# Three of seven block products of a mixture-of-experts second layer, taken one level deeper

## The chip, the cores and the metric

The kernel runs on one core of one Trainium2 chip. The metric is the device time of one launch in microseconds (us); less is better. A core has a matrix engine (TensorE, PE in the profile, with its weight loads as PEld), a vector engine (VectorE, DVE), a scalar engine (ScalarE, ACT), GpSimd (POOL) and SyncE (SP), which only issues transfers here. Each runs its own instructions in order, and they wait for each other by semaphores. On-chip data lies in SBUF, matmul results in banks of PSUM.

## The reference

A pre-norm block: attention with sine and cosine features, then a mixture of eight experts (E = 8) with the top two chosen for each token. Only the second half matters here. Every expert has room for 160 rows of each of 8 sequences, 1280 rows:

```python
h = jax.nn.relu(jnp.einsum('enc,ech->enh', buf, W1) + b1[:, None, :])   # C 512 -> H 2048
y = jnp.einsum('enh,ehc->enc', h, W2) + b2[:, None, :]                   # H 2048 -> C 512
y_tok = y.reshape(E * B * cap, C)[flat_idx.reshape(-1)].reshape(B, T * K, C)
y_tok = y_tok * (p_flat * keep.astype(x.dtype))[:, :, None]
return y_tok.reshape(B, T, K, C).sum(axis=2)
```

All of it is float32. The result is added to the residual x.

## The kernel before, in words

The first 1260 us are attention, normalisation and routing, which the change does not touch. Then come 16 chunks, two for each expert: even chunks (i = 0, 2, ...) of 768 rows (nh = 3) and odd chunks of 512 rows (nh = 2). A chunk is cut into two halves of rows, an upper and a lower one of nh blocks of 128 rows each, so that block number `block` of both halves can be handled together.

Both expert layers multiply 2 x 2 block matrices with seven products instead of eight (Strassen's scheme in Winograd's form). In the second layer the left matrix is `hid`: rows in two halves, the hidden 2048 in two halves of 1024 (NHQ = 8 pieces of 128). The right matrix is W2, 1024 + 1024 by 256 + 256 (DC = 256). The seven left operands and the seven right operands, called *parts* and *weights* 0 to 6, are made ahead by sums on VectorE: for the left side at the end of layer 1 (`p4`, lines 1280 to 1287), for the right side in `mix_w2` (lines 1066 to 1069).

`layer2(i, block, ...)` forms the two output tiles of one block, one from each half of the rows. Its `product` (line 1317) is a chain of 8 matmuls of 128 x 128 by 128 x 256 into one bank. The banks `top` and `mid` are accumulated over several products, and ScalarE copies or VectorE sums take what is needed from between (lines 1343 to 1369). Each finished row tile is multiplied by its gate on ScalarE (line 1329) and added to `out` in memory by an indirect transfer from POOL (line 1332). After each product, `next(aside)` advances `gather(i + 1)`, a generator that brings the rows of the next chunk: its transfers, a VectorE transpose for each tile of 128 rows (line 1175), and four sums (lines 1185 to 1188).

Layer 1 runs over q = 0 to 7. Each step has seven products p1 to p7 (line 1241), whose results ScalarE copies (lines 1251 to 1274) and whose weights are mixed by `mix_w1` (line 1214). p6 adds to the bank that p1 filled, so it needs ScalarE's copy of p1 (line 1251) first.

The order on TensorE, ScalarE, VectorE and SP is the order of the program text: `tc.manual_schedule` names these four engines. Tiles come from pools; a new tile of a pool with all its buffers taken waits for the last reader of the oldest. `hp` holds eight `hid` tiles, `w2p` eight tiles of W2, `yp` three row tiles y, `ps_p` six banks.

## Time and profile before

| | us |
|---|---|
| median of three runs | 3238.44 (3238.36 to 3239.85) |
| the profiled execution's own time | 3225.94 |
| its span, first to last instruction | 3224.2 |
| TensorE busy / VectorE / ScalarE / POOL | 3155.2 / 1936.5 / 1609.3 / 425.8 |
| mean granted clock of TensorE | 0.996 |
| second layer of an odd chunk (1712.70 to 1761.10) | 48.4 |
| second layer of an even chunk (1591.50 to 1664.30) | 72.8 |

The profile shows one execution. Busy times of engines overlap, so their sum is more than the span. [...] In a group line, the numbers after the bar are the busy time of the group in us, the mean length of one instruction in ns, and the idle time of the engine before them. In a timeline line they are start, length, engine, source line, operation, and how many were merged; what stands in brackets is the wait before and what ended it. In a line of stretches, each engine has its busy time and count, in the order PE, PEld, DVE, ACT, POOL, followed by the clock of TensorE, the share of the transfer engines, and GB/s.

### The profile page before, as it was taken

The numbers are of one execution on the slowest core, as the hardware profiler recorded it, in microseconds if no ns is written. First come the engines' busy times: TensorE is split into PE (matmuls) and PEld (weight loads), VectorE is DVE, ScalarE is ACT, GpSimd is POOL, SyncE is SP. The second block draws the span as 40 slices with busy tenths as digits, with TensorE's granted clock in tenths as the row PEclk, the third lists the DMA queues.
The fourth block names the chain that finished last, engine by engine and source line by source line (L and its number), as shares of the span: only waits on it lengthen the run. The fifth ranks groups of instructions, "written<-read, shape, count | busy, mean of one in ns | idle before, by whom it ended". The sixth has DMA issues, their size and how long they took to land.

```text
span 3224.2 us, 48128 instructions
## 1 busy us (share of the span) xinstructions
PE 3155.2 (98%) x18646; PEld 2136.9 (66%) x18646; DVE 1936.5 (60%) x4088; ACT 1609.3 (50%) x2289; POOL 425.8 (13%) x387
## 2 busy tenths in 40 slices
PE   5999999999999999999999999999999999999998
PEld 2444444444444445688688688688688688688687
DVE  8888888788787685634634634634634634634632
ACT  7888888888888875322322322322322322322322
POOL 3000202011111213311011011011011011011010
PEclk9999999999999999999999999999999999999999
DMA  5435454553545352434323333334333333334321
GB/s 165 145 99 164 133 147 141 146 157 106 184 106 158 96 165 87 129 78 108 121 66 104 122 66 104 123 64 106 122 66 102 123 66 103 123 66 104 119 46 20
DMA packets 288531, 358.52 MB, mean 111 GB/s; under 512 B 28376, under 2 KB 199088, under 8 KB 276272
## 3 DMA queue, kind: packets, MB, share of 16 engines
q1 hardware_dynamic: 264944, 312.20, 32.6%
q0 software_dynamic: 22912, 43.22, 7.5%
q8 instruction: 148, 2.42, 0.3%
q14 instruction: 79, 0.65, 0.1%
q10 hardware_dynamic: 448, 0.02, 0.0%
HBM read 207.02 MB, written 81.22 MB: 89 GB/s over the span
## 4 chain that ended last, share of the span: by engine, by line
PE 80%; DVE 3%; ACT 1%; issue 1%; DMA 0%; SPq 0%; POOLq 0%; DVEq 0%; ACTq 0%
PE ps_p L1241 30%; PE ps_p L1317 30%; PE av L717 9%; PE ps_s L683 9%; ACT e L703 1%; PE ps_s L215 1%; DVE qk_f L524 1%; PE ps_s L697 1%; DVE qk_r L447 0%; DMA qk<-qk_r 0%; DVE xT L837 0%; PE ps_s L874 0%; SPq L608 0%; PE ps_s L857 0%; DMA out_dram<-y,slots 0%
## 5 line engine op out<-in xcount | busy, mean ns | idle before, releaser
L703 ACT ACTIVATE e<-ps_s 128x1024 f32<-128x1024 f32 (+1 forms) x640 | 569.7, 937 | 184.2 <-PE ps_s L683 110.1
L683 PE MATMUL ps_s<-qk 64*128 64x512 f32 (+3 forms) x3072 | 598.1, 506 | 28.5 <-DMA qk<-qk_r 12.4
L1317 PE MATMUL ps_p<-w,hid 128*128 128x256 f32 x2560 | 575.9, 380 | 2.9 <-DVE w L1067 2.7
L1317 PEld LDWEIGHTS ps_p<-w,hid 128*128 128x128 f32 x2560 | 485.9, 190 | 74.9 <-DVE w L1067 7.6
L717 PE MATMUL av<-e,v 128*64 128x512 f32 (+3 forms) x3072 | 523.4, 490 | 0.0
L1317 PE MATMUL ps_p<-w_t,hid 128*128 128x256 f32 x1920 | 436.0, 380 | 0.5 <-DVE y L1366 0.5
L683 PEld LDWEIGHTS ps_s<-qk 64*128 64x128 f32 x3072 | 262.5, 188 | 216.2 <-issue 106.9
L1317 PEld LDWEIGHTS ps_p<-w_t,hid 128*128 128x128 f32 x1920 | 366.2, 191 | 51.1 <-DVE y L1366 0.9
L717 PEld LDWEIGHTS av<-e,v 128*64 128x64 f32 x3072 | 200.5, 137 | 283.0 <-issue 267.1
L1329 ACT ACTIVATE y<-y,slots 128x512 f32<-128x512 f32 x80 | 57.7, 722 | 524.5 <-DVE y L1362 448.2
L1241 PE MATMUL ps_p<-xe,w 128*128 128x256 f32 (+1 forms) x1024 | 317.6, 433 | 1.1 <-issue 1.1
L1241 PE MATMUL ps_p<-xe_s,t 128*128 128x256 f32 (+1 forms) x1024 | 318.2, 433 | 0.0
L1241 PE MATMUL ps_p<-xe,t 128*128 128x256 f32 (+1 forms) x1024 | 317.6, 433 | 0.0
L1332 POOL DMA_INDIRECT out_dram<-y,slots x80 | 127.4, 1593 | 1214.2 <-ACT y L1329 1055.6
L768 POOL DMA_INDIRECT slot_d<-token,slot x128 | 156.8, 1225 | 988.7 <-issue 612.2
L1241 PEld LDWEIGHTS ps_p<-xe_s,t 128*128 128x128 f32 x1024 | 193.7, 190 | 82.6 <-ACT hid L1251 1.6
L1241 PEld LDWEIGHTS ps_p<-xe,t 128*128 128x128 f32 x1024 | 194.2, 190 | 80.4 <-issue 0.4
L1241 PEld LDWEIGHTS ps_p<-xe,w 128*128 128x128 f32 x1024 | 194.2, 190 | 79.7 <-issue 1.2
L1343 DVE TENSOR_TENSOR y<-y,ps_p 128x256 f32<-128x256 f32 x40 | 16.9, 421 | 367.3 <-issue 191.4
L1284 DVE TENSOR_TENSOR hid<-hid 128x256 f32<-128x256 f32 (+1 forms) x128 | 64.0, 500 | 280.9 <-ACT hid L1282 280.9
L1241 PE MATMUL ps_p<-xe_s,w 128*128 128x256 f32 (+1 forms) x512 | 158.9, 433 | 0.6 <-ACT p L1257 0.6
L1251 ACT COPY hid<-ps_p 128x256 f32<-128x256 f32 (+1 forms) x128 | 54.3, 424 | 180.4 <-PE ps_p L1241 170.8
(229 smaller groups left out, 3640.6 us busy)
## 6 DMA issues: line engine op xcount, KB each, us to landing
w<-in_L_ffn_W_dram SPq DMA_DIRECT2D x256, 256.0 KB, 3.4
w<-in_L_ffn_W_dram SPq DMA_DIRECT2D x64, 512.0 KB, 8.1
qk<-qk_c SPq DMA_DIRECT2D x124, 256.0 KB, 4.4
qk<-qk_r SPq DMA_DIRECT2D x120, 256.0 KB, 4.8
qk_base<-base_d SPq DMA_DIRECT2D x28, 1024.0 KB, 7.7
xn_d<-xn SPq DMA_DIRECT2D x72, 256.0 KB, 2.4
rows_d<-xg SPq DMA_DIRECT2D x70, 256.0 KB, 2.1
x_mid<-in_L_attn_x_dram SPq DMA_DIRECT2D x16, 1024.0 KB, 8.9
```

Source lines behind the costliest of these rows:

```text
L215: nc.tensor.transpose(turned[:, a, :], src[r, :], ident[r, r])
L524: nc.vector.scalar_tensor_tensor(cols(p), ps[:, a, :].rearrange("p (t q) -> p t q", q=64), inv_qk[:, i * NCH + c : i * NCH + c + 1], cols( ...
L683: nc.tensor.matmul(ps[:, a, at : at + w], lhsT=pair[r, 1, kb * P : (kb + 1) * P], rhs=pair[r, 0, q0 : q0 + w], start=at == 0, stop=not own ...
L703: nc.scalar.activation(e, ps[:, :, :n], AF.Exp, scale=UNIT * UNIT / math.sqrt(2 * DH))
L717: nc.tensor.matmul(av[a * 64 : (a + 1) * 64, q0 - 512 * h :], lhsT=vt[:, kb, 2 * pr + a, :], rhs=es[i][:, a, at : at + w], start=kb == 0, ...
L768: queued = nc.gpsimd.indirect_dma_start(out=slot_d[b], out_offset=bass.IndirectOffsetOnAxis(ap=idx, axis=0), in_=src, in_offset=None,)
L1241: nc.tensor.matmul(ps, lhsT=weights[:, k, :], rhs=rows[:, k, :], start=first and k == 0, stop=last and k == 1, skip_group_check=True,)
L1251: nc.scalar.copy(self.blocks[0], self.top)
L1284: TT(g1, g3, h22, ALU.add)
L1317: nc.tensor.matmul(ps, lhsT=hs[k][:, part, cols], rhs=ws[k][weight], start=first and k == 0, stop=last and k == NHQ - 1, skip_group_check= ...
L1329: nc.scalar.activation(ys[r], ys[r], AF.Identity, scale=meta[:, e, jj[r], 1:2].bitcast(F32))
L1332: ins = nc.gpsimd.indirect_dma_start(out=out, out_offset=bass.IndirectOffsetOnAxis(ap=meta[:, e, jj[r], 0:1], axis=0), in_=ys[r], in_offse ...
```

## The change

For every chunk but the first, blocks 0 and 1 of the second layer are now handled together by a new function `layer2_quad`; block 2 of even chunks, and all of chunk 0, go through `layer2` as before. The pair has the same seven products, each for 256 rows. Four of them (0, 4, 5 and 6) stay plain: two chains of 8 matmuls with 256 columns. The other three (`SECOND`: part and weight 1, 2, and 3 with 6) are each cut into 2 x 2 blocks once more (rows 128 + 128, the inner 1024 in 512 + 512, columns 128 + 128) and done with seven chains of four matmuls with 128 columns. The sums of the operands, eight of 128 x 512, are made on VectorE by `mix`; ScalarE and VectorE combine the seven results in a tile c of four 128 x 128 blocks, which VectorE then adds to y. The order is: mix 0, products 0 and 4, second level 0, mix 1, product 5, second level 1, mix 2, product 6, second level 2.

The operand sums and c need room: in odd chunks the columns of `hid` that 512 rows leave free, in even chunks the tiles xe and xe_s, between their use by layer 1 and the next gather. So that slices can span pieces, `hid` and W2 become one tile each (all eight pieces), with the same transfers and sums. `yp` has four tiles instead of three. The gate of a lower row tile is applied to its two halves apart. In odd chunks the first mix of the next chunk's W1 comes before second level 2, and the gather's eight steps hang on the pair: two after product 0, two in each second level; in even chunks they hang on block 2.

```diff
     def load_w2(e):
-        w2_tiles[e] = []
+        w = w2_tiles[e] = pools["w2p"].tile([P, NHQ, 2, D], F32, name="w2")
         for k in range(NHQ):
-            w = pools["w2p"].tile([P, 2, D], F32, name="w2")
-            nc.sync.dma_start(w, src[:, :, k, :])
-            w2_tiles[e].append(w)
+            nc.sync.dma_start(w[:, k, :, :], src[:, :, k, :])
             yield
...
     def layer2(i, block, hid, aside):
...
+        gate(0, y1)
+        send(0, y1)
...
         TT(y22, y22, high, ALU.add)
+        gate(1, y22)
         product(top, 3, 6, False, True)
         TT(y21, top, low, ALU.add)
-        send(1)
+        gate(1, y21)
+        send(1, y2)
...
+    SECOND = [(1, 1), (2, 2), (3, 6)]
+
+    def layer2_quad(i, hid, aside, before_last):
...
+        def mix(n):
...
+            t1, t2, t3, t4, s2, s3, s4 = free[:7]
+            TT(t1, b12, b11, ALU.subtract)
+            TT(s3, a11, a21, ALU.subtract)
+            TT(a21, a21, a22, ALU.add)
+            TT(t2, b22, t1, ALU.subtract)
+            TT(s2, a21, a11, ALU.subtract)
+            TT(t3, b22, b12, ALU.subtract)
+            TT(s4, a12, s2, ALU.subtract)
+            TT(t4, b21, t2, ALU.subtract)
+            return (
+                (a11, b11), (a12, b21), (s4, b22), (a22, t4), (a21, t1), (s2, t2), (s3, t3)
+            )
...
+        def chain(ps, pair, first):
+            for k in range(4):
+                nc.tensor.matmul(
+                    ps, lhsT=pair[0][:, k, :], rhs=pair[1][:, k, :], start=first and k == 0,
+                    stop=k == 3, skip_group_check=True,
+                )
+
+        def second_level(n, pairs):
+            m1, m2, m3, m4, m5, m6, m7 = pairs
+            c = free[7 + n]
+            c11, c12, c21, c22 = (c[:, k, :] for k in range(4))
+            u, v, z = (bank()[:, :P] for _ in range(3))
+            chain(u, m1, True)
+            nc.scalar.copy(c11, u)
+            next(aside, None)
+            chain(v, m5, True)
+            nc.scalar.copy(c21, v)
+            chain(u, m6, False)
+            nc.scalar.copy(c12, u)
+            chain(z, m2, True)
+            TT(c11, c11, z, ALU.add)
+            chain(u, m7, False)
+            nc.scalar.copy(c22, u)
+            next(aside, None)
+            chain(v, m3, False)
+            TT(c22, c22, c21, ALU.add)
+            TT(c12, c12, v, ALU.add)
+            chain(u, m4, False)
+            nc.scalar.copy(c21, u)
+            return [c[:, 2 * b : 2 * b + 2, :] for b in two]
...
+        pairs = mix(0)
+        top, mid = bank(), bank()
...
+        product(top, 0, 0, True, False)
+        for b in two:
+            nc.scalar.copy(y11[b], of(top, b))
+            next(aside, None)
+        product(mid, 4, 3, True, True)
+        c = second_level(0, pairs)
+        for b in two:
+            TT(as_pair(y11[b]), as_pair(y11[b]), c[b], ALU.add)
+        pairs = mix(1)
+        product(top, 5, 4, False, False)
+        for b in two:
+            nc.scalar.copy(y12[b], of(top, b))
+            TT(y12[b], y12[b], of(mid, b), ALU.add)
+        c = second_level(1, pairs)
+        for b in two:
+            TT(as_pair(y12[b]), as_pair(y12[b]), c[b], ALU.add)
+        pairs = mix(2)
+        for b in two:
+            TT(y1[b], y1[b], b2_tiles[e], ALU.add)
+            gate[b](0, y1[b])
+            send[b](0, y1[b])
+        y2, y21, y22 = zip(*(new_y() for _ in two))
+        for b in two:
+            nc.scalar.copy(y22[b], of(mid, b))
+        product(top, 6, 5, False, True)
+        for b in two:
+            TT(y22[b], y22[b], of(top, b), ALU.add)
+            TT(y21[b], of(top, b), low, ALU.add)
+            TT(y22[b], y22[b], high, ALU.add)
+            gate[b](1, y22[b])
+        before_last()
+        c = second_level(2, pairs)
+        for b in two:
+            TT(as_pair(y21[b]), as_pair(y21[b]), c[b], ALU.add)
+            gate[b](1, y21[b])
+            send[b](1, y2[b])
...
     def experts(ending):
-        pools["hp"] = to_end.pool("hp", NHQ, **right)
+        pools["hp"] = to_end.pool("hp", 1, **right)
...
+            def mix_next():
+                if i + 1 < len(chunks):
+                    mix_w1(i + 1, 0)
+
+            if i:
+                layer2_quad(
+                    i, hid, iter(()) if nh > 2 else aside, mix_next if nh == 2 else lambda: None
+                )
+            for block in range(2 if i else 0, nh):
+                if block == nh - 1:
+                    mix_next()
+                layer2(i, block, hid, aside)
```

More of the change, by code (lines that the diff above doesn't have):

```diff
@@ L1052, in load_w2 @@
         src = W2[e].rearrange("(h k p) c -> p h k c", p=P, h=2)
-        w2_tiles[e] = []
+        w = w2_tiles[e] = pools["w2p"].tile([P, NHQ, 2, D], F32, name="w2")
         for k in range(NHQ):
-            w = pools["w2p"].tile([P, 2, D], F32, name="w2")
-            nc.sync.dma_start(w, src[:, :, k, :])
-            w2_tiles[e].append(w)
+            nc.sync.dma_start(w[:, k, :, :], src[:, :, k, :])
             yield
     def mix_w2(e):
-        for k, w in enumerate(w2_tiles[e]):
-            t = pools["w2p"].tile([P, 3, DC], F32, name="w2_t")
-            b11, b12 = w[:, 0, :DC], w[:, 0, DC:]
-            b21, b22 = w[:, 1, :DC], w[:, 1, DC:]
-            TT(t[:, 1, :], b12, b22, ALU.subtract)
-            TT(b12, b12, b11, ALU.subtract)
-            TT(t[:, 0, :], b22, b12, ALU.subtract)
-            TT(t[:, 2, :], b21, t[:, 0, :], ALU.subtract)
-            w2_tiles[e][k] = [b11, b21, b22, b12, t[:, 0, :], t[:, 1, :], t[:, 2, :]]
+        w = w2_tiles[e]
+        t = pools["w2p"].tile([P, NHQ, 3, DC], F32, name="w2_t")
+        b11, b12 = w[:, :, 0, :DC], w[:, :, 0, DC:]
+        b21, b22 = w[:, :, 1, :DC], w[:, :, 1, DC:]
+        t2, t3, t4 = (t[:, :, n, :] for n in range(3))
+        w2_tiles[e] = [b11, b21, b22, b12, t2, t3, t4]
+        for k in range(NHQ):
+            TT(t3[:, k, :], b12[:, k, :], b22[:, k, :], ALU.subtract)
+            TT(b12[:, k, :], b12[:, k, :], b11[:, k, :], ALU.subtract)
+            TT(t2[:, k, :], b22[:, k, :], b12[:, k, :], ALU.subtract)
+            TT(t4[:, k, :], b21[:, k, :], t2[:, k, :], ALU.subtract)
             yield
@@ L1220, in preln_attn_moe_kernel, with __init__ @@
     class Hidden:
-        def __init__(self, i, q, parts, asides):
+        def __init__(self, i, q, parts, hid, asides):
             e, j0, nh = chunks[i]
@@ L1227, in __init__ @@
             self.rows = parts
-            h = pools["hp"].tile([P, 7, HALF], F32, name="hid")
-            self.tile = h
-            self.blocks = [h[:, k, : self.n] for k in range(7)]
+            self.blocks = [hid[:, q, k, : self.n] for k in range(7)]
             self.low, self.high = (
@@ L1304, in layer1, with outputs, gate, send @@
         return this
-    def layer2(i, block, hs, aside):
+    def outputs(i, block):
         e, j0, nh = chunks[i]
+        jj = [j0 + block, j0 + nh + block]
+        def gate(r, part):
+            nc.scalar.activation(
+                part, part, AF.Identity, scale=meta[:, e, jj[r], 1:2].bitcast(F32)
+            )
+        def send(r, y):
+            ins = nc.gpsimd.indirect_dma_start(
+                out=out,
+                out_offset=bass.IndirectOffsetOnAxis(ap=meta[:, e, jj[r], 0:1], axis=0),
+                in_=y, in_offset=None, compute_op=ALU.add,
+            )
+            if i == 0:
+                tc.keep_in_program_order(ins)
+        return gate, send
+    def new_y():
+        y = pools["yp"].tile([P, D], F32, name="y")
+        return y, y[:, :DC], y[:, DC:]
+    def layer2(i, block, hid, aside):
+        e = chunks[i][0]
         ws = w2_tiles[e]
@@ L1317, in product @@
                 nc.tensor.matmul(
-                    ps, lhsT=hs[k][:, part, cols], rhs=ws[k][weight],
+                    ps, lhsT=hid[:, k, part, cols], rhs=ws[weight][:, k, :],
                     start=first and k == 0, stop=last and k == NHQ - 1, skip_group_check=True,
@@ L1321, in product @@
             next(aside, None)
-        jj = [j0 + block, j0 + nh + block]
-        ys = [pools["yp"].tile([P, D], F32, name="y") for _ in jj]
-        (y11, y12), (y21, y22) = ((y[:, :DC], y[:, DC:]) for y in ys)
+        gate, send = outputs(i, block)
+        (y1, y11, y12), (y2, y21, y22) = new_y(), new_y()
         low, high = b2_tiles[e][:, :DC], b2_tiles[e][:, DC:]
-        def send(r):
-            nc.scalar.activation(
-                ys[r], ys[r], AF.Identity, scale=meta[:, e, jj[r], 1:2].bitcast(F32)
-            )
-            ins = nc.gpsimd.indirect_dma_start(
-                out=out,
-                out_offset=bass.IndirectOffsetOnAxis(ap=meta[:, e, jj[r], 0:1], axis=0),
-                in_=ys[r], in_offset=None, compute_op=ALU.add,
-            )
-            if i == 0:
-                tc.keep_in_program_order(ins)
         def side_product():
@@ L1361, in layer2 @@
         TT(y12, y12, mid, ALU.add)
-        TT(ys[0], ys[0], b2_tiles[e], ALU.add)
-        send(0)
+        TT(y1, y1, b2_tiles[e], ALU.add)
+        gate(0, y1)
+        send(0, y1)
         if plain_first:
@@ L1367, in layer2, with places @@
         TT(y22, y22, high, ALU.add)
+        gate(1, y22)
         product(top, 3, 6, False, True)
         TT(y21, top, low, ALU.add)
-        send(1)
+        gate(1, y21)
+        send(1, y2)
+    def places(i, hid):
+        if chunks[i][2] == 2:
+            return [
+                hid[:, 4 * half : 4 * half + 4, part, 2 * P : 3 * P]
+                for part in range(7) for half in range(2)
+            ]
+        xe = pools["xep"].tile([P, NCH, 2, HALF], F32, name="xe")
+        s = pools["xep"].tile([P, 3, 2, HALF], F32, name="xe_s")
+        return [
+            t.rearrange("p a b n -> p (a b n)")[:, k * D : (k + 1) * D].rearrange(
+                "p (k n) -> p k n", n=P
+            )
+            for t, count in ((xe, 6), (s, 4))
+            for k in range(count)
+        ]
@@ new lines, in preln_attn_moe_kernel, with split, bank, as_pair @@
+    SECOND = [(1, 1), (2, 2), (3, 6)]
+    def layer2_quad(i, hid, aside, before_last):
+        e = chunks[i][0]
+        ws = w2_tiles[e]
+        free = places(i, hid)
+        low, high = b2_tiles[e][:, :DC], b2_tiles[e][:, DC:]
+        two = range(2)
+        def split(t, part_of):
+            return [[part_of(t[:, 4 * k : 4 * k + 4], c) for c in two] for k in two]
+        def mix(n):
+            part, weight = SECOND[n]
+            a = split(hid, lambda t, c: t[:, :, part, c * P : (c + 1) * P])
+            b = split(ws[weight], lambda t, c: t[:, :, c * P : (c + 1) * P])
+            (a11, a21), (a12, a22) = a
+            (b11, b12), (b21, b22) = b
+            t1, t2, t3, t4, s2, s3, s4 = free[:7]
[9 more added lines that the diff above has]
+                (a11, b11), (a12, b21), (s4, b22), (a22, t4), (a21, t1), (s2, t2), (s3, t3)
+            )
+        def bank():
+            return pools["ps_p"].tile([P, 512], F32, name="ps_p")
+        def chain(ps, pair, first):
[3 more added lines that the diff above has]
+                    stop=k == 3, skip_group_check=True,
+                )
+        def second_level(n, pairs):
[21 more added lines that the diff above has]
+            return [c[:, 2 * b : 2 * b + 2, :] for b in two]
+        def as_pair(t):
+            return t.rearrange("p (c n) -> p c n", n=P)
+        def product(ps, part, weight, first, last):
+            for b in two:
+                for k in range(NHQ):
+                    nc.tensor.matmul(
+                        ps[:, b * DC : (b + 1) * DC],
+                        lhsT=hid[:, k, part, b * P : (b + 1) * P], rhs=ws[weight][:, k, :],
+                        start=first and k == 0, stop=last and k == NHQ - 1,
+                        skip_group_check=True,
+                    )
+        gate, send = zip(*(outputs(i, b) for b in two))
+        pairs = mix(0)
+        top, mid = bank(), bank()
+        of = lambda ps, b: ps[:, b * DC : (b + 1) * DC]
+        y1, y11, y12 = zip(*(new_y() for _ in two))
+        product(top, 0, 0, True, False)
[30 more added lines that the diff above has]
+        c = second_level(2, pairs)
+        for b in two:
+            TT(as_pair(y21[b]), as_pair(y21[b]), c[b], ALU.add)
+            gate[b](1, y21[b])
+            send[b](1, y2[b])
@@ L1398, in experts @@
             parts, box = box[0], [None]
-            hs, tiles = [], None
+            hid = pools["hp"].tile([P, NHQ, 7, HALF], F32, name="hid")
+            tiles = None
             ahead = rows_ahead(i + 1) if i and i + 1 < len(chunks) else iter(())
@@ L1409, in experts @@
                 next(ahead, None)
-                tiles = layer1(Hidden(i, q, parts, [ending]), tiles, q == NHQ - 1)
-                hs.append(tiles.tile)
+                tiles = layer1(Hidden(i, q, parts, hid, [ending]), tiles, q == NHQ - 1)
                 if i == 0 and q == NHQ // 2:
@@ L1414, in experts @@
                     to_router.close()
-                    for name, bufs in (("w2p", NHQ), ("yp", 3), ("bp", 1)):
+                    for name, bufs in (("w2p", 1), ("yp", 4), ("bp", 1)):
                         pools[name] = to_end.pool(name, bufs, reuse_waits="tile", **left)
@@ L1430, in experts @@
                 aside = behind(2, aside)
-            for block in range(nh):
-                if block == nh - 1 and i + 1 < len(chunks):
+            def mix_next():
+                if i + 1 < len(chunks):
                     mix_w1(i + 1, 0)
-                layer2(i, block, hs, aside)
+            if i:
+                layer2_quad(
+                    i, hid, iter(()) if nh > 2 else aside, mix_next if nh == 2 else lambda: None
+                )
+            for block in range(2 if i else 0, nh):
+                if block == nh - 1:
+                    mix_next()
+                layer2(i, block, hid, aside)
             rest(aside)
```

## The prediction

> **What bounds the kernel now.** I read the page's busy shares and chain first, then the waits after 1420 us, where the expert stage runs undisturbed.

> ```profile
> PE 3155.2 (98%) x18646; PEld 2136.9 (66%) x18646; DVE 1936.5 (60%) x4088; ACT 1609.3 (50%) x2289; POOL 425.8 (13%) x387
> ...
> PE ps_p L1241 30%; PE ps_p L1317 30%; PE av L717 9%; PE ps_s L683 9%; ACT e L703 1%; PE ps_s L215 1%; DVE qk_f L524 1%; PE ps_s L697 1%; DVE qk_r L447 0%; DMA qk<-qk_r 0%; DVE xT L837 0%; PE ps_s L874 0%; SPq L608 0%; PE ps_s L857 0%; DMA out_dram<-y,slots 0%
> ```
> ```profile
> PEld ps_p L1317 <- DVE w L1067: 3.0, 7, 0.4
> ...
> PEld ps_p L1241 <- ACT hid L1251: 1.6, 8, 0.2
> ```

> TensorE is the bound: the two product lines hold 60% of the chain, and in 1800 us its weight loads wait 4.6 us in all. So every microsecond of matmul removed counts in full, and so does every wait that the change gives TensorE. Its price per instruction comes from the timeline:

> ```profile
> 1602.15 3.62 PE L1317 MATMUL ps_p<-w,hid 128*128 128x256 f32 x16
> 1605.60 0.38 PE L1317 MATMUL ps_p<-w_t,hid 128*128 128x256 f32 x1
> ```
> ```profile
> 1289.00 0.60 PE L828 MATMUL ps_t<-ident,xn 128*128 128x128 f32 x4
> ```
> ```profile
> 1292.12 0.41 PEld L857 LDWEIGHTS ps_t<-gather_e,lg 128*128 128x128 f32 x3
> ```

> Sixteen instructions fill 1602.15 to 1605.60: 0.216 us each at 256 columns. They are one block product, so each of the 8 matmuls of the code is two instructions (4480 in all for 40 blocks x 7 x 8). At 128 columns four take 0.60; the last one's own length is 0.27, so they start 0.109 apart. Full f32 weight loads behind tiny matmuls start (0.41-0.19)/2 = 0.11 apart.

> [...] here load and matmul would both need about 0.11 us and overlap. [...]

> ```profile
> 1350.90:1354.30 3.40, 1.84 (x7) 0.64 (x5) 3.19 (x9) 0.00 (x0) 1.55 (x2) 1.00 0.80 208
> 1354.30:1361.10 6.80, 5.66 (x13) 4.04 (x14) 3.35 (x9) 0.37 (x1) 0.00 (x0) 0.52 0.67 216
> ...
> 1289.40:1292.80 3.40, 2.67 (x19) 1.83 (x20) 2.59 (x6) 1.17 (x2) 1.77 (x3) 1.00 0.27 94
> ```

> The first number after the length is TensorE busy, the third from the end the clock. 1.56 us idle in one window cost 6.8 us at half clock, that is 3.4 us of work; 0.73 us idle cost none. [...]

> **What goes and what comes on TensorE.** Chunks 1 to 15 each get one pair by layer2_quad: 15 pairs, three products each, 45. Plain, such a product is 32 instructions x 0.216 = 6.91 us; second level it is 7 chains x 8 x 0.109 = 6.10 us (a chain 0.872). 0.81 x 45 = **36 us gained**. Bounds: at 0.112 each, 29 us; if load and matmul did not overlap at all (0.19), 56 x 0.08 x 45 = 200 us lost. The seven waits for L1067 go, since its product now starts 3.5 us later: about 2 us gained.

> **VectorE's price and its cover.**

> ```profile
> L1214 DVE TENSOR_TENSOR t<-w,t 128x256 f32<-128x256 f32 x244 | 102.9, 422 | 4.2
> ...
> L1175 DVE STREAM_TRANSPOSE xe<-z 128x512 f32<-128x512 f32 x32 | 33.5, 1084 | 0.0
> ...
> L1187 DVE TENSOR_TENSOR xe_s<-xe 128x768 f32<-128x768 f32 x7 | 6.7, 958 | 0.2
> ...
> L1185 DVE TENSOR_TENSOR xe_s<-xe 128x512 f32<-128x512 f32 x8 | 5.5, 693 | 0.3
> ```

> Starts lie closer than lengths: in the timeline 0.61 us apart at 512 (3209.26 and 3209.87) and 0.34 at 256 (1714.69 and 1715.03) where nothing is passed on, 0.035 more than the length where a sum needs the one before it. A mix is eight sums of 512, seven starts of 0.61 or once 0.73 and a last length: 5.1 us. Mix 0 has the two plain products before it as cover (13.8 us), even behind VectorE's backlog in even chunks (last hidden sums and two w2 mixes, until 1599.0 where layer 2 began at 1591.5: 7.5 us). Mix 1 has 6.9 us of product. Both fit. Inside a second level, a chain waits for a ScalarE copy of the bank: 0.20 from chain's end to its reader (1664.31 to 1664.51), 0.27 for the copy (372 at 256, 478 at 384, so an estimate of 266 at 128), 0.05 back to a weight load (1665.95 to 1666.00): 0.52 against 0.87 of other chain. Fits, if ScalarE is free.

> **Where it does not fit, first place.** At the third second level, ScalarE's copies stand behind the gates of y22. Count from E, when TensorE starts product(top, 6, 5). VectorE adds c to y12 until E+0.9, mix 2 runs E+0.84 to 5.9, the two b2 sums start at 5.84 and 6.45 (0.69 each). ScalarE gates both y1 (0.72 each, 0.63 apart) from 6.57 to 7.92 (ScalarE's own overlap is 0.10: 1713.30 and 1713.70 for lengths of 0.50), then copies mid to both y22: 8.47. VectorE can only now do its six sums of 256 (0.34 apart): 8.24 to 10.36. The last gate is done at 10.89, the copy of c11 at 11.06. TensorE reached the third second level at E+6.91 and wants that bank after two chains, at 8.65; it gets it at 11.06 plus wake-up and load 0.16. **2.56 us lost in each of 15 pairs: 38 us.** Bounds: 1.2 us if VectorE were on time, 3.2 if its waits cost more.

> **Second place: odd chunks.** There the gather of the next chunk's rows has eight steps hung on the pair; the eighth comes inside the third second level, with one transpose (1.1) and four sums of 768 (0.99 apart), ahead of the sums that end c and y21 and of the gates. mix_w1 (1.6 us) and another transpose fit into the stall before. From the end of chain m2: 0.2 + 0.29 + 1.1 + 4.0 + 0.5 + 0.7 + gates 1.0 = 7.2, and ScalarE's copy of the next chunk's p1 0.5: 7.7 us. TensorE needs that copy at p6, after three chains and p1, p5 (1.29 each): 5.2. With 0.16 for waking, **2.6 us lost**, 7 times: 18 us; bounds 0 and 3.5.

> **Third: the clock.** [...] Fifteen stalls x 0.8 x 3.41 = **40 us**. At half clock the odd chunks' second stall shrinks from 2.6 to about 0.7, because its VectorE work doesn't slow down; with its own clock losses that leaves 12 us instead of 18. Bounds: 0, and 60.

> **Rest.** The w2 and hid tiles in one piece issue the same DMAs on SP; old readers end before the next writes except for y21's sum, already in the second place. The extra y gates are shorter ones. POOL sends one by one:

> ```profile
> 3210.99 1.55 POOL L1332 DMA_INDIRECT out_dram<-y,slots  x1 [17.17 <-ACT y L1329]
> 3216.57 1.56 POOL L1332 DMA_INDIRECT out_dram<-y,slots  x1 [4.03 <-DMA out_dram<-y,slots]
> ```

> The second waited for the first to land, 5.6 us. With both last sends after the end of TensorE the tail grows from 12.2 to about 14 us: 2 us lost. Elsewhere nobody waits: four y tiles cover it, and the next chunk's first fetch on POOL, some 3 us later, has a 9 us q step.

> **Sum.** -36 - 2 + 38 + 12 + 40 + 2 = +54 us. Against the profiled execution's 3225.9 this is 3280; the median of the runs shown is 12.5 us above that execution, which nothing here explains, so I put the sum on it: 3238.4 + 54 = **3292**. One measurement can tell about 0.2%, 6.5 us.

> **Rivals.** (a) The stalls come, the clock stays up: -36 - 2 + 38 + 18 + 2 = +20, 3259. [...] Against: the window at 1350.9. (b) *Faster*: the stall in the third second level is the one mechanism. If y22's sums and gates are done by E+8.2, the copy of c11 is in time; then no stall, no clock loss, and -38 + 2 + at most 18 from the odd chunks: 3203 to 3220. It turns to a gain below about 1.2 us of stall[...]. Against it: mix 2 alone ends at E+5.9, and two b2 sums, two gates, two copies, six sums and two gates follow in line. (c) Weight loads set the pace at 128 columns[...]: the gain is gone, +50 to +200 more, 3340 and up. Against: 0.109 and 0.11 above. (d) The pairs don't reach the second level, so no gain and no stalls: within 0.2%; the code calls it for every i but 0.

> **Chances.** Forecast 0.52, (a) 0.20, (b) 0.15, (c) 0.06, (d) 0.07, where I count also that gains and stalls cancel. Faster 0.15, same 0.07, slower 0.78. The forecast's own range, from the bounds of stall and clock, is 3262 to 3320. For 8 in 10 I take 3222 to 3325: it reaches over (a) and (d) and leaves out most of (b) and (c).

> **What would show it.** Right: L1317's old 380 ns rows fall by 1440, and 2520 of 128 columns appear, starting 0.109 apart; TensorE waits about 2.5 us for ScalarE's c11 copy at each third second level and at p6 of even chunks; the clock falls to 0.5 for 6.8 us after many of these; VectorE stays under 85% in the pairs. Wrong: no wait there (then the order in ScalarE's queue is not as read, and the result is (b)), 128-column instructions spaced above 0.115, or waits at m5 to m3 of the first two second levels, which would mean that a mix is late.

## The result, and the profile after

The changed kernel takes 3278.99 us (median of four runs, 3277.45 to 3279.95), the kernel before 3238.52 us (four runs, 3238.36 to 3239.85). The ratio is 1.0124, interval 1.0106 to 1.0141: 40 us slower. The forecast was 3292, in the range 3222 to 3325.

The page of the kernel after, busy shares and the chain by engine, then the chain of the kernel before:

```profile
PE 3151.3 (96%) x19726; PEld 2165.0 (66%) x19726; DVE 2211.1 (68%) x4643; ACT 1665.7 (51%) x2554; POOL 424.7 (13%) x387
...
PE 76%; DVE 5%; ACT 2%; issue 1%; DMA 1%; SPq 0%; POOLq 0%; DVEq 0%; ACTq 0%
```
```profile
PE 80%; DVE 3%; ACT 1%; issue 1%; DMA 0%; SPq 0%; POOLq 0%; DVEq 0%; ACTq 0%
```

TensorE is busy for 96% of the span (98% before), and VectorE and ScalarE now hold 7% of the chain (4% before). Who made TensorE wait is in the waits of the kernel after from 1430 us on (us in total, times, longest):

```profile
PE ps_p L1439 <- ACT hid L1450: 16.8, 8, 2.1
PE ps_p L1439 <- ACT xe_s L1450: 14.7, 7, 2.1
PE ps_p L1239 <- ACT hid L1249: 12.1, 6, 2.3
PE ps_p L1239 <- DMA w<-in_L_ffn_W_dram: 1.1, 1, 1.1
```

Line 1439 is `chain`, line 1450 the copy of c11, lines 1239 and 1249 are layer 1's products and the copy of p1. The first two lines are one wait in each of the 15 pairs; c11 lies in `hid` in odd chunks and in xe_s in even ones. The third is the wait at p6, at six of the seven boundaries (a boundary is the step from the pair of an odd chunk to layer 1 of the next chunk). The fourth is p6 at the seventh boundary: there the view names a transfer, but the weight load just ahead of that matmul waited for the same copy, L1249. Before, this list held no wait of TensorE's matmuls at all after 1420 us.

The two profiled executions differ ahead of chunk 1, which starts at 1422.5 us before and at 1435.3 after. Chunk 0's layer 1 took 82.6 us in the one and 90.2 in the other. This goes with the chip, it seems, and not with the change: all four traces from chip 6 below have 82.6 there, those from chips 2 and 15 have 89.8 to 93.7, and the kernel before has medians of 3225.5 on chip 6 and of 3237.8 and 3238.6 on the others. (The chips of the two executions themselves are not on record.) It would also account for the 12.5 us that the prediction could not explain. So I compare the traces from the start of chunk 1: 1801.7 us before, 1840.4 after, 38.7 more, nearly all of the measured 40. In each experiment below both kernels ran on the same chip, so ratios are the measure there.

In the table, and from here on, the time of a stage runs from the start of its first matmul to that of the next stage. A wait costs a little more so measured than the waits above show (2.36 us for 2.1), mostly because they count idle time between shown lengths, and an instruction of 128 columns is shown for 0.275 us where the next starts 0.112 after it. A clock drop is a stretch in which the trace has TensorE's granted clock at 0.5.

| from chunk 1 on, us | forecast | in the trace |
|---|---|---|
| 45 products at 6.25 instead of 6.91 | -36 | -29.5 |
| old waits for L1067, and for L1251 | -2 | -2.6 |
| 15 waits before the third second level goes on, 2.36 each | +38 | +35.4 |
| 7 waits at p6, 1.4 to 2.7 each | +12 | +15.1 |
| clock drops, 11 of 1.63 | +40 | +18 |
| tail after the end of the last matmul, 14.3 instead of 12.1 | +2 | +2.2 |
| sum | +54 | +38.6 |

The pair of an odd chunk takes 46.38 us without a wait (in kernels below), 48.74 here with the wait alone and 50.37 with a drop behind it: so 2.36 and 1.63. Ten of the eleven drops follow the wait in a third second level, and one follows the wait at p6.

The first wait, step by step, in the timeline of the kernel after (first pair, chunk 1; E is 1516.88):

```profile
1522.66 1.28 DVE L1504 TENSOR_TENSOR y<-y,b_b 128x512 f32<-128x512 f32 x2
1523.38 1.33 ACT L1310 ACTIVATE y<-y,slots 128x512 f32<-128x512 f32 x2 [6.04 <-DVE y L1504]
...
1524.62 0.62 ACT L1509 COPY y<-ps_p 128x256 f32<-128x256 f32 x2
1524.68 1.06 PE L1439 MATMUL ps_p<-hid 128*128 128x128 f32 x8
1525.00 0.42 DVE L1512 TENSOR_TENSOR y<-y,ps_p 128x256 f32<-128x256 f32 x1 [1.06 <-ACT y L1509]
...
1526.67 0.41 DVE L1514 TENSOR_TENSOR y<-y,b_b 128x256 f32<-128x256 f32 x1
...
1527.12 0.51 ACT L1310 ACTIVATE y<-y,slots 128x256 f32<-128x256 f32 x1 [0.49 <-DVE y L1514]
...
1527.54 0.24 ACT L1450 COPY hid<-ps_p 128x128 f32<-128x128 f32 x1
...
1527.84 1.97 PE L1439 MATMUL ps_p<-hid 128*128 128x128 f32 x8 [2.10 <-ACT hid L1450]
```

Read it backwards. TensorE goes on at 1527.84, when c11 has been copied (1527.78). The copy stood behind the last gate of y22, that gate waited for VectorE's last sum of 256, VectorE's six sums waited for the copies to y22, those stood behind the gates of y1, and these waited for the b2 sums behind mix 2. The chain of m1 was done at 1524.68, nearly 3 us before its copy began: the data was there, but ScalarE's queue had not come to it.

The wait at p6, at the boundary that follows:

```profile
1531.83 1.10 DVE L1175 STREAM_TRANSPOSE xe<-xe_s 128x512 f32<-128x512 f32 x1
...
1535.94 0.96 DVE L1188 TENSOR_TENSOR xe_s<-xe,xe_s 128x768 f32<-128x768 f32 x1
1536.82 0.28 DVE L1462 TENSOR_TENSOR hid<-hid 128x128 f32<-128x128 f32 x1
...
1537.19 0.27 ACT L1465 COPY hid<-ps_p 128x128 f32<-128x128 f32 x1 [4.48 <-DVE hid L1462]
...
1537.79 0.91 ACT L1310 ACTIVATE y<-y,slots 128x256 f32<-128x256 f32 x2 [0.34 <-DVE y L1519]
...
1538.60 0.46 ACT L1249 COPY hid<-ps_p 128x384 f32<-128x384 f32 x1
...
1539.11 1.56 PE L1239 MATMUL ps_p<-xe_s,t 128*128 128x384 f32 x4 [2.33 <-ACT hid L1249]
```

VectorE is at the gather's last transpose and its sums from 1531.83 to 1536.90. Only then come the sums of c; ScalarE's copy into c21 (which has to wait until the old c21 has been added to c22) and the gates follow, and behind them the copy of p1.

Second levels without a wait show the pace:

```profile
1746.47 1.95 PE L1439 MATMUL ps_p<-hid 128*128 128x128 f32 x16
1748.26 1.06 PE L1439 MATMUL ps_p<-w,hid 128*128 128x128 f32 x8
```

Sixteen instructions from 1746.47 to 1748.26: 0.112 us each.

### The profile page after: what moved, and what is told of

It reads as the page before. It is cut to its first block, busy times and chain, and to the rows that moved or that the text cites. A ratio compares the mean times of both kernels' runs of the same rounds, so it can differ in the third digit from the quotient of the medians.

```text
span 3275.7 us, 51300 instructions
## 1 busy us (share of the span) xinstructions
PE 3151.3 (96%) x19726; PEld 2165.0 (66%) x19726; DVE 2211.1 (68%) x4643; ACT 1665.7 (51%) x2554; POOL 424.7 (13%) x387
## 4 chain that ended last, share of the span: by engine, by line
PE 76%; DVE 5%; ACT 2%; issue 1%; DMA 1%; SPq 0%; POOLq 0%; DVEq 0%; ACTq 0%
PE ps_p L1239 29%; PE ps_p L1474 12%; PE av L717 9%; PE ps_s L683 9%; PE ps_p L1439 8%; PE ps_p L1340 7%; ACT y L1310 1%; PE ps_s L215 1%; ACT e L703 1%; PE ps_s L697 1%; DVE qk_f L524 1%; DVE qk_r L447 0%; DVE y L1514 0%; DVE y L1512 0%; DVE y L1504 0%
## 5 line engine op out<-in xcount | busy, mean ns | idle before, releaser
L703 ACT ACTIVATE e<-ps_s 128x1024 f32<-128x1024 f32 (+1 forms) x640 | 569.9, 937 | 189.3 <-PE ps_s L683 110.3
L683 PE MATMUL ps_s<-qk 64*128 64x512 f32 (+3 forms) x3072 | 599.0, 506 | 32.8 <-DMA qk<-qk_r 12.4
L717 PE MATMUL av<-e,v 128*64 128x512 f32 (+3 forms) x3072 | 524.0, 490 | 0.0
L683 PEld LDWEIGHTS ps_s<-qk 64*128 64x128 f32 x3072 | 262.3, 187 | 221.2 <-issue 108.7
L717 PEld LDWEIGHTS av<-e,v 128*64 128x64 f32 x3072 | 200.6, 137 | 284.3 <-issue 268.0
L1239 PE MATMUL ps_p<-xe_s,t 128*128 128x256 f32 (+1 forms) x1024 | 321.0, 436 | 17.9 <-ACT hid L1249 12.1
L1474 PE MATMUL ps_p<-w_t,hid 128*128 128x256 f32 x960 | 212.2, 379 | 0.0
L1474 PE MATMUL ps_p<-w,hid 128*128 128x256 f32 x960 | 209.7, 379 | 0.0
L1474 PEld LDWEIGHTS ps_p<-w,hid 128*128 128x128 f32 x960 | 182.4, 190 | 26.3
L1474 PEld LDWEIGHTS ps_p<-w_t,hid 128*128 128x128 f32 x960 | 180.1, 190 | 23.2
L1310 ACT ACTIVATE y<-y,slots 128x256 f32<-128x256 f32 (+1 forms) x120 | 66.2, 576 | 239.1 <-DVE y L1372 111.0
L1249 ACT COPY hid<-ps_p 128x256 f32<-128x256 f32 (+1 forms) x128 | 54.2, 423 | 186.5 <-PE ps_p L1239 169.7
L1340 PE MATMUL ps_p<-w,hid 128*128 128x256 f32 x640 | 144.8, 381 | 2.5 <-DVE w L1068 2.5
```

Of the source, the lines that this page charges most:

```text
L683: nc.tensor.matmul(ps[:, a, at : at + w], lhsT=pair[r, 1, kb * P : (kb + 1) * P], rhs=pair[r, 0, q0 : q0 + w], start=at == 0, stop=not own ...
L703: nc.scalar.activation(e, ps[:, :, :n], AF.Exp, scale=UNIT * UNIT / math.sqrt(2 * DH))
L717: nc.tensor.matmul(av[a * 64 : (a + 1) * 64, q0 - 512 * h :], lhsT=vt[:, kb, 2 * pr + a, :], rhs=es[i][:, a, at : at + w], start=kb == 0, ...
L1239: nc.tensor.matmul(ps, lhsT=weights[:, k, :], rhs=rows[:, k, :], start=first and k == 0, stop=last and k == 1, skip_group_check=True,)
L1249: nc.scalar.copy(self.blocks[0], self.top)
L1310: nc.scalar.activation(part, part, AF.Identity, scale=meta[:, e, jj[r], 1:2].bitcast(F32))
```

## The experiments

### Gates of y22 behind the third second level; gather earlier; both

```diff
# e1_gates_late
             TT(y22[b], y22[b], high, ALU.add)
-            gate[b](1, y22[b])
         before_last()
         c = second_level(2, pairs)
+        for b in two:
+            gate[b](1, y22[b])
         for b in two:
# e2_gather_early
         product(mid, 4, 3, True, True)
+        for _ in range(3):
+            next(aside, None)
         c = second_level(0, pairs)
# e3_both: both edits
```

**e1_gates_late.** 

> Both gates of y22 stand behind the third second level in ScalarE's queue; nothing else moves. Theory (order in ScalarE's queue): the 2.36 us wait for the copy of c11 vanishes in all 15 pairs (-35 us) with its clock drops (-17). In odd chunks VectorE's chain to the end of the pair is late by its own work and keeps its place in time, so TensorE reaches p6 of the next chunk earlier and waits there about 4 us instead of 2.1 (+14, and up to 12 for clock drops there). Sum near 3252, 3240 to 3262. Rival (VectorE has too much to do in a pair, the queue order only shows it): a wait of over 1 us appears in second levels elsewhere, even chunks included, and the time stays above 3265.

Measured: ratio 1.0034 (1.0021 to 1.0046); the expected 3252 against 3238.5 is 1.0042. Waits of TensorE from 1430 us on:

```profile
PE ps_p L1239 <- ACT hid L1249: 20.6, 7, 2.9
PE ps_p L1239 <- DVE xe L1186: 9.1, 7, 1.3
```

No second level waits any more; layer 2 of odd chunks takes 46.4 us and of even chunks 70.6, the least of all kernels here. The boundaries now wait in two places, 1.3 us at p5 (which needs the gather's sum of L1186) and 2.9 at p6, and layer 1 of an even chunk takes 77.0 us instead of 72.2: VectorE kept its place in time and TensorE came earlier, as expected. Not as expected: these 4.2 us of idle time cost only one clock drop in 7, and the tail is 18.4 us instead of 14.3, because TensorE ends sooner and the last sends do not.

**e2_gather_early.** 

> The gather's steps three to five are hung on product 4, so its eighth step, with the four sums, falls into the second of the three second levels. Theory: the wait at p6 of even chunks (2.1 us, 7 times) goes and with it one clock drop; the 2.36 us waits at the third second level stay as they are: 3279 - 15 - 2 = 3262, 3257 to 3268. Rival (the end of an odd pair is late because of the late third second level itself, not of the gather): under 5 us gained, the wait at p6 stays above 1.5 us.

Measured: ratio 1.0103 (1.0086 to 1.012), expected 1.0073. The waits at p6 are gone (layer 1 of all even chunks 72.24 us, as before), but the third second levels of odd chunks wait longer. Chunk 1 in the timeline of this kernel:

```profile
1509.76 1.06 PE L1439 MATMUL ps_p<-hid 128*128 128x128 f32 x8
1513.49 1.16 PE L1439 MATMUL ps_p<-hid 128*128 128x128 f32 x8 [2.67 <-ACT hid L1450]
```

I had hung the gather's four sums on the second of the second levels, where they stand ahead of the sums for c and y12 and so of mix 2; that made the late chain in odd chunks later by 0.6 us. Also 14 of the 15 pairs had a clock drop instead of 10. So the rival fails, since the gather was the cause at p6, and the theory was wrong in that the other waits did not stay as they were: the new place was a bad one.

**e3_both.** 

> Both moves together. Theory: no wait of TensorE above 0.3 us is left in the expert stage after chunk 0, no clock drop after 1435 us; left are the 15 x 3 x 0.66 us gained on TensorE (-30), 2 for the old waits, +2 for the tail: 3238.5 - 30 = 3209, 3204 to 3216. Rival (too much work for VectorE): waits of 20 us or more in sum are left, 3230 or above. Rival (the clock falls because of the dense 128-column instructions, not of the waits): about ten drops to 0.5 are left, 3209 + 17 = 3226.

Measured: ratio 0.993 (0.9913 to 0.9946), expected 0.9909; the changed kernel becomes faster than before. One wait is left:

```profile
PE ps_p L1439 <- ACT hid L1450: 2.1, 7, 0.3
```

It makes layer 2 of seven odd chunks 46.95 us instead of 46.38. It fits the delay of mix 2 seen in e2, now through y1's gates alone; no run separates it. There is no clock drop after 1435 us until the last matmul, with the same 2520 instructions of 128 columns: the drops come from the waits, not from dense narrow matmuls. The rest of what is missing against the 3209 expected is in the tail, 18.8 us instead of 14.3: the four sends of the last pair are strung one after another from y1's gates on, 5.5 to 5.7 us apart, and TensorE now ends sooner than they do.

### The pair without a second level

```diff
# e4_plain_pair (shortened; n = 0, 1, 2; no mix)
-        c = second_level(n, pairs)
+        side = bank()
+        product(side, *SECOND[n], True, True)
+        for _ in two:
+            next(aside, None)
+        c = [side[:, b * DC : (b + 1) * DC] for b in two]
# e7_halves: each of these products as two halves of 128 columns (shortened)
+        side = bank()
+        for b in two:
+            for h in two:
+                for k in range(NHQ):
+                    nc.tensor.matmul(
+                        side[:, b * DC + h * P : b * DC + (h + 1) * P],
+                        lhsT=hid[:, k, part, b * P : (b + 1) * P],
+                        rhs=ws[weight][:, k, h * P : (h + 1) * P],
+                        start=k == 0, stop=k == NHQ - 1, skip_group_check=True,
+                    )
```

**e4_plain_pair.** 

> The pair as it is, with its order, gates and tiles, but its three second levels are plain products into one bank, without operand sums. Theory: the structure of the pair costs nothing by itself: before's TensorE time less the old waits (-2) plus the longer tail (+2): 3238, 3234 to 3243. Rival (taking two blocks together, one tile for hid and W2, or the split gates cost time): 3248 or more, with waits of TensorE at the joints of products.

Measured: ratio 1.0044 (1.0027 to 1.0061), 14 us slower than before, not equal. Layer 2 takes 48.35 us in odd chunks, as before, and 72.52 in even ones (72.82 before, with the old waits for L1067), so taking two blocks together costs nothing there. All of the loss is one wait, and the tail of 14.5 us:

```profile
PE ps_p L1239 <- ACT hid L1249: 12.8, 7, 1.8
```

The p6 wait (2.1 us of lost time at each of 7 boundaries) thus does not need the second level or VectorE's operand sums. This kernel, too, hangs the gather's last step on the pair's last product, which my expectation had forgotten; that this step is the cause was shown by e2, and e8 below shows it again.

**e7_halves.** 

> The pair with plain products instead of the second level (no operand sums), and those three products issued as 64 instructions of 128 columns each instead of 32 of 256. It measures the price of 128 columns with plain operands. If 0.1117 us is what such an instruction with a full weight load costs, each of the 45 products takes 7.15 instead of 6.91 us: +11 us on the kernel with plain pairs, layer 2 of an odd chunk 49.1 instead of 48.35. If the operands or waits of the second level made it slow and the bare price is 0.109: +3 us, 48.55.

Measured: ratio 1.0079 (1.0062 to 1.0096), layer 2 of odd chunks 49.06 us, so 0.24 us more than in e4 for each of three products: (6.91 + 0.237) / 64 = 0.1117 us for an instruction of 128 columns with plain operands. That is the 0.112 of the second level: its pace is the price of the shape, not of its sums, waits or accumulation.

### Taking the lateness alone

```diff
# e5_y1_first
+        for b in two:
+            TT(y1[b], y1[b], b2_tiles[e], ALU.add)
+            gate[b](0, y1[b])
+            send[b](0, y1[b])
         pairs = mix(2)
-        for b in two:
-            TT(y1[b], y1[b], b2_tiles[e], ALU.add)
-            gate[b](0, y1[b])
-            send[b](0, y1[b])
# e8_gather_five
         product(mid, 4, 3, True, True)
+        for _ in range(5):
+            next(aside, None)
         c = second_level(0, pairs)
```

**e5_y1_first.** 

> The two b2 sums of y1, their gates and sends stand ahead of mix 2 instead of behind it; the gates of y22 stay ahead of the third second level. If the wait for c11 is the sum of two things, VectorE late by mix 2 and the gates' place, the lateness goes: the six sums then start when product 6 ends (E+7.1), the last gate is done at 9.75, c11's copy at 9.93, and TensorE waits 1.4 us instead of 2.36 in each of the 15 pairs (-15 us). The clock theory (a 3.41 us window in which TensorE works under about 0.37) expects no drop for 1.4 us of idling (-18 us), where a theory that any wait may cost a drop expects most of the eleven to stay. Ratio to before 1.0023 with no drops, 1.0075 with drops. Layer 2 of even chunks: 71.95 us. The wait at p6 of even chunks stays.

Measured: ratio 1.0048 (1.0031 to 1.0065), between the two. Layer 2 of even chunks takes 71.96 us, as worked out. Waits:

```profile
PE ps_p L1239 <- ACT hid L1249: 16.4, 7, 2.4
PE ps_p L1439 <- ACT hid L1450: 9.1, 8, 1.1
PE ps_p L1439 <- ACT xe_s L1450: 8.0, 7, 1.1
```

Layer 2 of odd chunks takes 47.79 us, 1.41 over the 46.38 without a wait. So the 2.36 us are two parts: about 1.0 from VectorE and ScalarE being late with mix 2 and y1, 1.4 from the place of the gates, which stays. None of the 15 shorter waits cost a drop; the two drops of this run fell at p6, where layer 1 of two chunks took 76.55 us and of the other five 74.86. The ratio is above the 1.0023 worked out because of these two drops and because TensorE, earlier now, loses 2.6 us at p6 (74.86 against 72.24 before) instead of 2.1 or so.

**e8_gather_five.** 

> Only the gather moves: steps three to seven hang on product 4, so that the eighth, with its four sums, falls into the first second level, far from mix 2. Theory: the 7 waits at p6 of even chunks go (-15 us), and the third second level of odd chunks keeps its wait of 2.36 us, because the sums no longer delay mix 2, as they did when they fell into the second of the three (2.9 us and more). Clock drops between 7 and 15, depending on where the stalls fall in the windows; windows with TensorE at work under 0.37 of the time have one, others none. Ratio to before 1.0075, 1.005 to 1.0095. Rival (moving the gather only moves the wait): 1.010 or above, as with three steps.

Measured: ratio 1.0075 (1.0058 to 1.0092). The p6 waits are gone. The third second levels wait as in the changed kernel (the view has the same two lines, 16.8 us in 8 and 14.7 in 7), and ten of these waits cost a drop. Moving the gather does not by itself move the wait; its place in e2 did.

### Three moves

```diff
# e6_three_moves: y1 first as in e5, five steps as in e8, and
-        def second_level(n, pairs):
+        def second_level(n, pairs, between=lambda: None):
...
             nc.scalar.copy(c22, u)
+            between()
...
-            gate[b](1, y22[b])
         before_last()
-        c = second_level(2, pairs)
+        c = second_level(2, pairs, lambda: [gate[b](1, y22[b]) for b in two])
```

**e6_three_moves.** 

> Three moves: y1's sums and gates ahead of mix 2; the gates of y22 in ScalarE's free time inside the third second level (after the copy of c22); gather steps three to seven hung on product 4, so that the eighth falls into the first second level. Theory: no wait of TensorE of over 0.1 us after chunk 0 and no clock drop; against the kernel with two moves (ratio 0.993) the 7 waits of 0.5 us in odd chunks go (-4) and the last sends start 4 to 5 us sooner: ratio 0.9903, about 31 us under before. Layer 2: 46.4 us odd, 70.6 even. Rival (the sends, or VectorE's load in the first second level, take up the gain): 0.993 or above.

Measured: 3208.2 us against 3237.79 for the kernel before on that chip, ratio 0.9917 (0.99 to 0.9933), expected 0.9903: faster than both kernels. From chunk 1 on it takes 1771.5 us, 30.2 less than before, which is the -29.5 and -2.6 of the table and 1.8 of a longer tail. The list of TensorE's waits after 1430 us is empty. The third second level of chunk 1 and the boundary, where 2.1 and 2.3 us were lost:

```profile
1523.73 1.95 PE L1439 MATMUL ps_p<-hid 128*128 128x128 f32 x16
1525.52 1.06 PE L1439 MATMUL ps_p<-w_t,hid 128*128 128x128 f32 x8
...
1530.38 1.45 PE L1239 MATMUL ps_p<-xe,t 128*128 128x384 f32 x4
1531.67 1.45 PE L1239 MATMUL ps_p<-xe_s,t 128*128 128x384 f32 x4
```

No line has a wait behind it. The kernel has the same sums on VectorE as the changed one, so their number was not the limit; the order was.

## Why the prediction was right, and where its sizes were off

**The bound and the gain.** TensorE was the bound (busy for 98% of the span before), and the second level saved 0.66 us in each of 45 products. The term of 36 us came out as 29.5: an instruction of 128 columns takes 0.1117 us, not 0.109. I had both numbers before me: the tiny matmuls behind full weight loads were 0.11 apart, and my lower end of 29 us used 0.112. The 0.109 came from transposes, whose weight loads are shorter (0.14 against 0.19 us in the groups of the kernel before). I should have taken a row with the same load.

**The covers of mix 0 and mix 1, and the waits inside the first two second levels,** held: 6.25 us each, no wait.

**The first place.** The ledger's times held to 0.16 us at every step (c11's copy done at E+10.90, forecast 11.06; last sum of y22 at E+10.20, forecast 10.36), and TensorE went on 0.06 after that copy, not 0.16. 35.4 us for 38. That order on ScalarE is the cause was shown by e1, that the lateness is 1.0 of it by e5.

**The second place.** The cause named, the gather's eighth step at the end of the pair, was right: e2 and e8 show it, and e4 shows that it needs no second level. The sizes: at the six boundaries with a drop shortly before, 1.4 to 2.6 us were lost, where the forecast had 0.7 (it had counted on drops of 6.8 us, and these lasted 3.4; that VectorE's work does not slow down in them held, with 1.10 us for the transpose at 1528.47, in a drop, and 1.11 at 1511.90, outside); at the one without, 2.7 (layer 1 took 76.55 us, with 1.6 of its own drop), where it had 2.6. That makes 15.1 us for 12. The 0.29 in the list stands for a sum of 128 columns, which the trace before does not have; an estimate from its groups (692 ns at 512, 422 at 256) is 287 ns, and the trace after has 265 to 292. The 2.6 owes something to a slip: the steps listed there add up to 7.8 and 8.3, not to 7.2 and 7.7, and 8.3 would have given 3.2. In the trace the chain takes 7.7 us (chunk 9: from 2516.59 to p1's copy at 2524.32), because the steps overlap more than the list has it.

**The clock.** This term was the one most mis-sized: 18 us for 40. In each of the two traces the granted clock changes only on one grid of 3.413 us (before at 1354.63 and 1361.46, after at 1527.99 and 1531.40, for example); a step of that grid is a window below. Drops were as many as feared (11 for 12), but each lasted 3.41 us, not 6.8, and cost 1.63. That the count came out is partly luck: 0.8 drops for each stall was my estimate, with the place of a stall in the windows taken as random, and waits of nearly the same length gave 14 drops in e2. The drop in the trace before on which the forecast rested spans two windows (6.83 us); its second window had two further waits in it, which may be why. And my stretch was laid 0.3 us off: that drop begins at 1354.63. Read again on the grid, in stretches of the kernel before, then after (twice), then e1:

```profile
1351.22:1354.63 3.41, 1.52 (x5) 0.59 (x4) 3.20 (x9) 0.00 (x0) 1.23 (x2) 1.00 0.79 225
1354.63:1358.04 3.41, 2.60 (x5) 1.68 (x6) 3.05 (x8) 0.12 (x1) 0.00 (x0) 0.50 0.70 237
```
```profile
1650.87:1654.28 3.41, 1.31 (x12) 1.23 (x12) 1.44 (x5) 1.37 (x5) 0.35 (x1) 1.00 0.62 77
1654.28:1657.69 3.41, 3.41 (x19) 3.41 (x18) 0.29 (x1) 0.44 (x2) 1.58 (x1) 0.50 0.20 10
```
```profile
1896.63:1900.04 3.41, 1.46 (x14) 1.27 (x12) 2.08 (x6) 2.04 (x7) 1.62 (x1) 1.00 0.36 31
1900.04:1903.45 3.41, 3.26 (x29) 3.26 (x30) 0.29 (x1) 0.80 (x4) 1.11 (x1) 1.00 0.28 50
```
```profile
1765.01:1768.42 3.41, 1.56 (x4) 0.68 (x4) 3.31 (x7) 0.73 (x3) 0.00 (x0) 1.00 1.01 343
1768.42:1771.83 3.41, 1.86 (x6) 1.20 (x7) 1.60 (x5) 2.14 (x6) 0.00 (x0) 1.00 0.82 229
```

**Tail.** As forecast: 2.2 us for 2.

**The sum.** 22 us too much for the clock and 6.5 too much gain have opposite signs and partly cancel: the total of the trace was 15 us off, the clock alone 22. **The range** was right to reach below the forecast; rival (a), no drops, would have given 3259, and the result lies between it and the forecast.

## What to carry to other kernels

Before adding work to a kernel that one engine bounds, write down what stands in the in-order queue of each helper engine at the moment the bound engine needs it: here three small reorderings, with no sum less, turned 1.2% slower into 0.8% faster. A copy that frees a bank should not stand behind an operation that waits for a third engine: that place alone cost 1.4 us in each pair of e5. And hang the last step of a side task where its engine has time, not where the loop happens to end.

## What the runs showed that I had not expected

The chunks repeat almost in step with the grid of clock windows: in e2 and e8 most drops came 122.9 us apart, 36 windows of 3.413 us. So equal or nearly equal waits cost ten or fourteen drops of 15 in three kernels (the changed one, e8 and e2), and the longer waits at the boundaries one of 7 in another (e1). Such a count is no independent sample, and a change of a few tenths of a us elsewhere may shift it by several drops, each worth 1.63 us. Where the line lies between 0.37 and 0.40 of a window at work, or whether a finer measure decides, stays open. A drop after one thin window, with full work behind it, lasted one window: 3.41 us for each of the eleven in the changed kernel.
